# Splitting the last grouped FFN into three parts of token tiles and routing two of them inside the attention ahead of it

## The chip, the cores and the metric

The kernel runs on one core of one Trainium2 chip. The core has five engines that work from queues of their own, each in order: PE (matrix multiplication and transposes; its weight loads are listed apart as PEld), DVE (vector work), ACT (activation functions and copies), POOL (which also issues the indirect DMAs, those that scatter or gather rows by an index) and SP (which issues the plain DMAs). The metric is the time of one execution on the device, in microseconds (us). Three executions of the kernel before took 4240.65, 4247.43 and 4250.56 us, so the median is 4247.43 us.

## The reference, cut to what matters

The input is 8 sequences of 512 tokens of 256 numbers, 4096 tokens in all, in float32. Six blocks follow one another, each adding to the tokens: an expert FFN, a causal attention, the same expert FFN, a grouped FFN, a second attention without a mask, and the same grouped FFN again. The change concerns the last two:

```python
def _L1_attn_ref(x, w_q, w_k, w_v, w_o):            # 16 heads of 64
    q, k, v = (jnp.einsum('bsd,hdk->bhsk', x, w) for w in (w_q, w_k, w_v))
    weights = jax.nn.softmax(jnp.einsum('bhqk,bhmk->bhqm', q, k) * scale, axis=-1)
    z = jnp.einsum('bhqm,bhmk->bhqk', weights, v)
    ...
    return x + jnp.einsum('bse,ed->bsd', z, w_o)

def _L1_ffn_ref(x, gate_w, w1, w2, w3, ws1, ws2, ws3):
    weights, indices = _gate(xt, gate_w)             # 4 of 16 experts, from 2 of 4 groups
    ...
    a = jax.nn.silu(h1) * h3                         # each expert: 256 -> 128
    y = jnp.einsum('tei,eid,te->td', a, w2, c)       # only 4 of 16 in c are not zero
    z = jax.nn.silu(xt @ ws1) * (xt @ ws3) @ ws2     # a shared FFN for every token
    return (y + z).reshape(shape)

x = x + _L1_attn_ref(_layernorm(x, axis=-1), ...)
x = x + 0.5 * _L1_ffn_ref(_layernorm(x, axis=-1), ...)
```

## The kernel before

The tokens stay on chip in the tile `x`, as 32 token tiles of 128 tokens. Most of the text below is on two stages.

**The second attention** (`_attn1`) runs over 64 chunks n, 8 for each of the 8 sequences, each with two heads, and each in two halves g = 2n and 2n+1. A half computes scores, takes the maximum (DVE, L1110), the exponentials (ACT, L1117), divides (DVE, L1127), transposes (PE, L1139) and copies the transposes back (L202 on ACT, L204 on DVE). What doesn't belong to the chain of a chunk is cut into small pieces: the list `fill` holds projections, value products and the units of `Front`, and is emptied over the chunk; `own[n]` holds pieces that run at the end of chunk n (the statistics of layer normalisation, `moments`, and their end, `ln_finish`); `advance(steps, 1)` runs one more piece of a routing and is called six times a chunk. The order of the instructions of each engine is the order in which this code writes them, but for some statistics which the scheduler moves ahead.

**The grouped FFN** (class `Grouped`) sends each token's normalised row to four slots in DRAM, one for each expert chosen. Slots are collected into 144 slot tiles of 128 rows that have one expert each. The token tiles are dealt into parts, before 20 and 12 of them. For each part the routing (`routing`) finds experts, weights and slots: a long sequence of small DVE instructions with three PE matmuls in it (L1426, L1434, L1514), cut by `yield` into pieces. Then `send` (L1358, the DMA on L1364) issues four indirect DMAs a token tile. When all rows of a part have been sent, the slot tiles that these rows must fill can be computed, and `closed` says up to which tile that is. `ready` says how many tiles must be done and stored before the results of a part's tokens may be fetched. For parts of 20 and 12, `closed` is 0 and 65, and `ready` is 96 and 144.

**The steps.** `tile_steps` gives one step for each slot tile, 144, and four to empty the pipeline. A step transposes a tile (`turn`, L1768 `tpx`, copied by ACT to `xT`, L1770), multiplies the tile before it with its expert's weights (`hide`, L1786 `hs`, then ACT L1792 and DVE L1794), transposes that of three steps before (`back`, L1798 `tpa`, copied by ACT, L1800) and gives the result of four steps before (`give`, L1806 `yps`), which is copied out by ACT or DVE:

```python
            if j < self.closed[-1] and len(self.parts) > 2:

                nc.scalar.copy(ys["at"][:, i, :], yp)
            else:
                nc.vector.tensor_copy(ys["at"][:, i, :], yp)
```

Slot tiles come in by plain DMAs (`load`, L1752) in groups of up to four, and go out to DRAM by plain DMAs (L1818), all on SP's queue. A group of the next part is not loaded two groups ahead (L1780).

**The way back.** `collect` (L1571) makes a list of pieces. A piece issues one indirect DMA on POOL that gathers a tile of result rows (`gather`, L1546, tile `yg`, eight buffers, at most four transfers at a time), and adds the rows gathered two token tiles earlier to `x` (`add`, DVE, L1565). There are 128 gathers.

**The last stage** (`ffn1_after`) is what runs after the attention. It loads the weights, normalises and transposes the tiles of part 1 (`prepare`), and then runs the 148 steps. Beside each of the first ones two pieces of part 1's routing run, and at their end part 1's sends are written in one go, 48 of them. From step `f.ready[0] + 6` on, which is step 102, each step also takes one or two pieces of the way back. After the steps comes the tail: a `Pump` runs the shared FFN, 48 units (L1702 `hp`, L1724 `yp`), and takes pieces of the way back by the pattern on L2045, ten for six units, until none is left. Each token tile goes out when its shared part and its rows are in.

**Part 0** is prepared inside the attention by `Front`: `units` normalises a group of four tiles (POOL, L1354), transposes it and computes the gate's logits, and `send` normalises a tile again and sends it. The chunk after which this may begin is `begin = NC * groups + 2`, 42 for the 20 tiles: units in chunks 43 to 47, routing from chunk 48, one tile sent in each half of chunks 54 to 63.

Of the kernel before, what the change touches and what calls it, by code (L numbers as in the profile page):

```python
# [20 lines left out]
P = 128  # L21
# [40 lines left out]
class Kernel:  # L62
# [951 lines left out]
    def _attn1(self, ctx, weights, beside, after):  # L1014
# [169 lines left out]
            t = psum.tile([P, CH], F32, name="row", tag="m", bufs=3)  # L1184
            return t[:, :cols]

        known = []
        steps = after.routing(0, front.lg, front.pool, row_psum, lambda: known.append(True))
        groups = after.parts[0] // QT

        def moments(pool, stats, t):
            return lambda: self.ln_moments(pool, stats, t, 2)
# [2 lines left out]
        own = {}  # L1195
        for first, tiles, n in ((3 * QT, 2 * QT, 10), (5 * QT, 3 * QT, 25)):
            for t in range(0, tiles, 2):
                own[n] = moments(pool, stats, first + t)
                n += 1
            own[n] = lambda first=first, tiles=tiles: self.ln_finish(pool, stats, first, tiles)  # L1200

        begin = NC * groups + 2
        for t in range(0, after.parts[0], 2):
            own[33 + t // 2] = moments(front.pool, after.stats, t)
        assert len(own) == 4 + 6 + 2 + after.parts[0] // 2 and max(own) == begin
        last = own[begin]
        own[begin] = lambda: (last(), self.ln_finish(front.pool, after.stats, 0, after.parts[0]))

        E = mybir.EngineType
        with tc.manual_schedule(engines={E.PE, E.DVE, E.Activation, E.Pool}):  # L1210
            self.ln_range(pool, stats, 0, 3 * QT)
            for piece in sum(prepare(0), []) + heads(0) + heads(1):
                piece()
            exps, divide = scores(0)
            exps(1)
            divide(0)
            divide(1)
            fill, tail = [], []
            coming = prepare(1)
            for n in range(N):  # L1220
                b, c = divmod(n, NC)
                if c == 0:
                    coming = prepare(b + 1) if b + 1 < B else [[]] * NC
                if n + 2 < N:
                    fill += heads(n + 2)
                fill += coming[c]
                if 1 <= n - begin <= groups:
                    fill += front.units(n - begin - 1, row_psum)

                def rest():  # L1230

                    if beside:
                        beside.pop(0)()

                def ahead():

                    if n > begin + groups:
                        advance(steps, 1)

                for half in range(2):  # L1240
                    g = 2 * n + half
                    if g + 1 < 2 * N:
                        exps, divide = scores(g + 1)
                    if half == 0 and tail:
                        tail.pop(0)()
                    t = g - 2 * N + after.parts[0]
                    if t >= 0:
                        assert known
                        front.send(t)
                    turn(n, 2 * half)  # L1250
                    more = g + 1 < 2 * N
                    if more:
                        exps(1)
                    if half == 0 and tail:
                        tail.pop(0)()
# [12 lines left out]
                    rest()  # L1268
                    ahead()
                if n in own:  # L1270
                    own[n]()
# [659 lines left out]
class Front:  # L1931


    def __init__(self, k, f, ctx):
        self.k, self.f = k, f
        self.pool = ctx.enter_context(k.tc.tile_pool(name="front", bufs=1, reuse_waits="tile"))
        self.gw = self.pool.tile([P, DC, E1], F32, name="gw")
        k.nc.sync.dma_start(out=self.gw, in_=k.w["gate_wT"].rearrange("(c p) e -> p c e", p=P))
        self.lg = self.pool.tile([P, f.parts[0], E1], F32, name="chosen")
        self.xn = {}  # L1940

    def normal(self, t, n):
# [4 lines left out]
            self.f.rows(self.k.nc.gpsimd, self.xn[:, i, :], t - t % QT + i)  # L1947
        return self.xn

    def units(self, g, row_psum):  # L1950

        k, nc = self.k, self.k.nc
        xn = self.normal(g * QT, QT)
        xnT = self.pool.tile([P, DC, CH], F32, name="xnT")

        def column(c):
            def run():
                tp = row_psum(CH)
                for i in range(QT):
                    nc.tensor.transpose(tp[:, i * P : i * P + P], xn[:, i, c * P : c * P + P], k.ident)  # L1960
                k.evict(xnT[:, c, :], tp, c)
            return run

        def logits():
            lp = row_psum(CH)
            for c in range(DC):
                nc.tensor.matmul(
                    lp[0:E1, :], lhsT=self.gw[:, c, :], rhs=xnT[:, c, :], start=(c == 0), stop=(c == DC - 1)
                )
            lT = self.pool.tile([E1, CH], F32, name="lT")  # L1970
            nc.scalar.copy(lT, lp[0:E1, :])
            box.append(lT)

        def back():
            lg = row_psum(QT * E1).rearrange("p (t e) -> p t e", e=E1)
            for i in range(QT):
                nc.tensor.transpose(lg[:, i, :], box[0][:, i * P : i * P + P], k.ident[0:E1, 0:E1])
            nc.vector.tensor_copy(self.lg[:, g * QT : g * QT + QT, :], lg)

        box = []  # L1980
        return [column(c) for c in range(DC)] + [logits, back]

    def send(self, t):
        self.f.send(0, t, self.normal(t, 1)[:, t % QT, :])


def ffn1_after(k, f, out):
# [3 lines left out]
    rows_out = out.rearrange("(t p) d -> p t d", p=P)  # L1991
    with ExitStack() as ctx, k.tc.manual_schedule(engines={E.PE, E.DVE, E.Activation, E.Pool, E.SP}):
        f.enter(ctx)
        a = f.parts[0]
        load, step, total = f.tile_steps()
        f.expert_weights()
        load(0)
        f.shared_weights()
        part = f.prepare(1)
        while advance(part, 1):  # L2000
            pass
        part = f.route_and_send(1)
        left = {t: 2 for t in range(TT)}

        def done(t):
            left[t] -= 1
            if left[t] == 0:
                nc.sync.dma_start(out=rows_out[:, t, :], in_=k.x[:, t, :])

        coming = f.collect(done)  # L2010
        begin = f.ready[0] + 6
        rest, more = list(range(a // QT)), True
        for i in range(total):
            step(i)
# [36 lines left out]

def tile_kernel(tc, w, out):
    with ExitStack() as ctx:
# [89 lines left out]
```

## Time and profile before

| what | value |
|---|---|
| median of three runs | 4247.43 us |
| the profiled execution, its own time | 4227.88 us |
| its span, first to last instruction | 4226.2 us |
| busy: PE, DVE, ACT, POOL | 3723.0, 2115.9, 1484.4, 1203.4 us |
| mean granted clock of PE | 0.916 |
| score matmuls of the second attention | from 2528.9 us, the last chunk's at 3714.0 us |
| weights of the last stage are asked for | 3734.8 us |
| first slot tile of the last stage is transposed | 3764.3 us |
| first and last send of part 1 | 3802.0 and 3863.5 us |
| first and last gather of the last stage | 4006.9 and 4205.6 us |
| first shared matmul of the tail | 4108.0 us |

Times inside the execution are from its first instruction on. A busy time counts overlapping instructions once. "Idle before, releaser" in brackets is how long an engine had done nothing when an instruction began, and what seems to have ended that. "Issue" there means that the profile shows nothing waited for, "remote" that the event came from something it has no record of.

### The profile page before, as it was taken

Reading aid. Unit: us, or ns where it says so; the run is one execution under the profiler, and the core shown is the slowest. Engines: PE = TensorE matmul, PEld = TensorE weight load, DVE = VectorE, ACT = ScalarE, POOL = GpSimd, SP = SyncE. Lnnn points to the kernel's source line nnn. Section 1 sums busy time; section 2 is a strip of 40 time slices with the busy share of each in tenths; the row PEclk is TensorE's granted clock in tenths of the full one; section 3 lists DMA queues with packets and bytes.
Section 4 is the critical chain, followed back from the end, with each engine's and each line's share of the span. In section 5 each row is a group of like instructions: output and inputs, shape, how many; then the busy total and the mean of one; then the engine's idle time right before and its main releaser. Section 6 shows DMA issues by size and latency. Waiting matters only on the chain.

```text
span 4226.2 us, 51448 instructions
## 1 busy us (share of the span) xinstructions
PE 3723.0 (88%) x17088; PEld 2154.2 (51%) x17088; DVE 2115.9 (50%) x5708; ACT 1484.4 (35%) x3483; POOL 1203.4 (28%) x1098
## 2 busy tenths in 40 slices
PE   4999978999999499997567989999999999985987
PEld 2666643333334266664245764555554544554754
DVE  7122126554544622213442458786777678662354
ACT  3222223343343322222132435454454444442431
POOL 2433342232230143331533332210000113604065
PEclk7999988898896699999688999999999999997998
DMA  5333247200000323324222741000000000234453
GB/s 190 65 79 77 51 118 242 86 25 12 21 23 3 101 66 77 76 53 118 83 93 99 235 129 31 28 23 1 1 1 1 1 1 31 70 107 140 156 175 109
DMA packets 262995, 316.64 MB, mean 75 GB/s; under 512 B 31696, under 2 KB 232784, under 8 KB 262480
## 3 DMA queue, kind: packets, MB, share of 16 engines
q1 hardware_dynamic: 213584, 212.12, 15.7%
q0 software_dynamic: 49152, 101.24, 9.9%
q8 instruction: 142, 2.33, 0.2%
q14 instruction: 117, 0.96, 0.1%
HBM read 157.81 MB, written 147.06 MB: 72 GB/s over the span
## 4 chain that ended last, share of the span: by engine, by line
PE 64%; issue 13%; DVE 10%; ACT 5%; POOL 3%; another core or an unknown queue 3%; DMA 2%; SPq 0%; POOLq 0%; ACTq 0%; DVEq 0%
PE hs L1786 6%; PE hp L518 5%; PE op L531 5%; PE zp L1153 5%; PE sp L1105 5%; PE tp L1139 5%; PE pq L1080 4%; PE st L853 3%; PE yps L1806 3%; PE hp L1702 3%; PE yp L1172 3%; PE pv L1060 3%; POOL acc_d L538 2%; PE pp L721 2%
## 5 line engine op out<-in xcount | busy, mean ns | idle before, releaser
L1117 ACT ACTIVATE ex<-sp,nmax 128x512 f32<-128x512 f32 x512 | 344.8, 685 | 469.4 <-DVE nmax L1110 463.3
L531 PE MATMUL op<-w,hid 128*128 128x256 f32 x2048 | 456.2, 380 | 0.0
L518 PE MATMUL hp<-exT,w 128*128 128x512 f32 x1024 | 448.9, 597 | 0.0
L1546 POOL DMA_INDIRECT yg<-ys_d,slot x256 | 265.7, 1038 | 565.7 <-DMA ys_d<-ys 209.8
L531 PEld LDWEIGHTS op<-w,hid 128*128 128x128 f32 x2048 | 384.9, 190 | 57.0 <-issue 7.7
L1786 PE MATMUL hs<-w_sb,xT 128*128 (+1 forms) x1152 | 320.6, 403 | 61.3 <-ACT xT L1770 30.5
L538 POOL DMA_INDIRECT acc_d<-ob,idx x128 | 207.0, 1617 | 570.9 <-ACT ob L537 570.9
L536 DVE TENSOR_TENSOR ob<-op,b 128x256 f32<-128x256 f32 x128 | 54.4, 425 | 542.7 <-PE op L531 465.6
L1139 PEld LDWEIGHTS tp<-ident,ex 128*128 128x128 f32 x2048 | 228.7, 141 | 183.0 <-issue 107.5
L518 PEld LDWEIGHTS hp<-exT,w 128*128 128x128 f32 x1024 | 193.5, 191 | 232.3 <-issue 230.4
L824 DVE CUSTOM_DVE_ANT_0 junk<-sp,mask 128x128 f32<-128x128 f32 (+3 forms) x512 | 248.6, 485 | 124.9 <-PE sp L817 104.7
L1110 DVE TENSOR_REDUCE nmax<-sp 128x2 f32<-128x1024 f32 x256 | 300.3, 1215 | 17.8 <-PE sp L1105 16.5
L1139 PE MATMUL tp<-ident,ex 128*128 128x128 f32 x2048 | 279.4, 279 | 13.8 <-DVE eT L204 12.9
L522 ACT ACTIVATE hid<-hp,b 128x512 f32<-128x512 f32 x256 | 175.9, 687 | 323.0 <-PE hp L518 305.5
L1364 POOL DMA_INDIRECT slots_d<-wide,slot x176 | 173.4, 985 | 340.5 <-DVE lane L1501 232.3
L1105 PE MATMUL sp<-qk,qk 64*128 64x512 f32 x1024 | 257.4, 621 | 2.1 <-ACT ex L1117 2.1
L862 ACT ACTIVATE ex<-st 128x1024 f32<-128x1024 f32 (+3 forms) x256 | 174.2, 703 | 240.6 <-DVE st L860 240.4
L1786 PEld LDWEIGHTS hs<-w_sb,xT 128*128 128x128 f32 x1152 | 207.9, 201 | 93.0 <-ACT xT L1770 35.7
L1127 DVE TENSOR_SCALAR ex<-ex,rec 128x512 f32<-128x512 f32 x512 | 246.0, 523 | 8.8
L1080 PE MATMUL pq<-xnT,wide 128*128 128x512 f32 x512 | 241.7, 596 | 5.5 <-ACT qk L1086 5.5
L1794 DVE TENSOR_TENSOR as<-sgs,hs 128x128 f32<-128x128 f32 x288 | 82.5, 286 | 309.0 <-ACT sgs L1792 234.4
L1153 PE MATMUL zp<-eT,v 128*64 128x512 f32 x1024 | 234.9, 599 | 0.0
(346 smaller groups left out, 5866.7 us busy)
## 6 DMA issues: line engine op xcount, KB each, us to landing
xs<-slots_d SPq DMA_DIRECT2D x70, 512.0 KB
ys_d<-ys SPq DMA_DIRECT2D x70, 512.0 KB
w<-in_W SPq DMA_DIRECT2D x32, 1024.0 KB
slots_d<-mask SPq DMA_DIRECT2D x8, 2304.0 KB
ys_d<-mask SPq DMA_DIRECT2D x8, 2304.0 KB
w_sb<-in_w SPq DMA_DIRECT2D x24, 512.0 KB
xn_d<-xn SPq DMA_DIRECT2D x16, 512.0 KB
acc_d<-x SPq DMA_DIRECT2D x8, 1024.0 KB
```

What stands on the lines that cost most here:

```text
L518: nc.tensor.matmul(hp, lhsT=w1[:, c, f * P : f * P + P], rhs=exT[e][:, c, h * CH : h * CH + CH], start=(c == 0), stop=(c == DC - 1),)
L531: nc.tensor.matmul(op, lhsT=hid[h][:, f, i * P : i * P + P], rhs=w2[:, f, :], start=(f == 0), stop=(f == FC - 1),)
L538: inst = nc.gpsimd.indirect_dma_start(out=acc_d[:, :], out_offset=bass.IndirectOffsetOnAxis(ap=idx[:, e, st : st + 1], axis=0), in_=ob, in ...
L824: nc.vector.tensor_tensor_reduce(out=junk[:, :wd], in0=sps[h // 2][:, h % 2, :wd], in1=mask[:, S - wd :], scale=1.0, scalar=NEG, op0=ALU.a ...
L1080: nc.tensor.matmul(pp, lhsT=(wq, wk)[a][:, k, c * P : c * P + P], rhs=seq[b]["xnT"][:, k, :], start=(k == 0), stop=(k == DC - 1),)
L1105: nc.tensor.matmul(sp[:, j, :], lhsT=q[r, qt * P : qt * P + P], rhs=k[r, :], start=True, stop=True)
L1110: nc.vector.tensor_reduce(m, sp, AX.X, ALU.max, negate=True)
L1117: nc.scalar.activation(ch["ex", 2 * half + i][:, j, :], sps[i][:, j, :], AF.Exp, bias=nmax[i][:, j : j + 1], accum_out=sums[i][:, j : j + 1],)
L1139: nc.tensor.transpose(tp[:, k, :], ch["ex", qt][:, j, k * P : k * P + P], self.ident)
L1153: nc.tensor.matmul(zp[DK1 * j : DK1 * j + DK1, :], lhsT=seq[b]["v", h][:, k, at : at + DK1], rhs=ch["eT"][:, j, k, :], start=(k == 0), sto ...
L1546: inst = nc.gpsimd.indirect_dma_start(out=self.y[t, r], out_offset=None, in_=self.k.ys_d[:, :], in_offset=bass.IndirectOffsetOnAxis(ap=sel ...
L1786: nc.tensor.matmul(hp.rearrange("p a i -> p (a i)"), lhsT=st[j]["xT"][:, c, :], rhs=self.w13[:, st[j]["e"], c, :].rearrange("p e i -> p (e ...
```

## The change

The last grouped FFN gets three parts of 12, 8 and 12 token tiles. The first two are prepared inside the attention, each on its own schedule, and the third takes the place of the former part 1. `closed` becomes 0, 33 and 49, `ready` 65, 112 and 144. In the attention part 0 has its units in chunks 27 to 29, its routing from chunk 30 and its sends in halves 96 to 107; part 1 has its units in chunks 43 and 44, its routing from chunk 45 and its sends in halves 112 to 119. The statistics move to chunks 11 to 26 and 35 to 42. In the last stage the way back starts at the step that the next token tile's part allows: tiles 0 to 11 from step 71, tiles 12 to 19 from step 118, and tiles 20 to 31 after the steps. Because there are now more than two parts, the condition on L1812 quoted above holds for the first 49 slot tiles.

```diff
-        known = []
-        steps = after.routing(0, front.lg, front.pool, row_psum, lambda: known.append(True))
-        groups = after.parts[0] // QT
+        known, steps = {}, {}
+        ahead_of = [(h, NC * after.base[h + 1] // QT + 2) for h in range(len(after.parts) - 1)]
+        sends = {}
+        for h, begin in ahead_of:
+            steps[h] = after.routing(h, front.lg[h], front.pool, row_psum, lambda h=h: known.setdefault(h, True))
+        at = 2 * N - 4
+        for h, _ in reversed(ahead_of):
+            at -= after.parts[h] + 4
+            for t in range(after.parts[h]):
+                sends[at + t] = (h, t)
...
-        begin = NC * groups + 2
-        for t in range(0, after.parts[0], 2):
-            own[33 + t // 2] = moments(front.pool, after.stats, t)
+        for h, begin in ahead_of:
+            first, tiles = after.base[h], after.parts[h]
+            for t in range(first, first + tiles, 2):
+                n = NC * (t // QT + 1) + 2
+                own.setdefault(min(n + 1 + t % QT, begin), []).append(moments(front.pool, after.stats, t))
+            own[begin].append(
+                lambda first=first, tiles=tiles: self.ln_finish(front.pool, after.stats, first, tiles)
+            )
...
-                if 1 <= n - begin <= groups:
-                    fill += front.units(n - begin - 1, row_psum)
+                for h, begin in ahead_of:
+                    if 1 <= n - begin <= after.parts[h] // QT:
+                        fill += front.units(h, n - begin - 1, row_psum)
...
-                    if n > begin + groups:
-                        advance(steps, 1)
+                    for h, begin in ahead_of:
+                        if n > begin + after.parts[h] // QT:
+                            advance(steps[h], 1)
...
-                    t = g - 2 * N + after.parts[0]
-                    if t >= 0:
-                        assert known
-                        front.send(t)
+                    if g in sends:
+                        h, t = sends[g]
+                        assert h in known
+                        front.send(h, t)
...
-        part = f.prepare(1)
+        part = f.prepare(last)
...
-        begin = f.ready[0] + 6
         rest, more = list(range(a // QT)), True
+
+        def begin():
+
+            t = (TT + 2) - -(-len(coming) // TOPK)
+            return f.ready[sum(t >= b for b in f.base[1:-1])] + 6
+
         for i in range(total):
             step(i)
             more = more and advance(part, 2)
             if not more and rest and i % 4 == 0:
                 f.normal(rest.pop(0))
-            if i >= begin:
-                for _ in range(1 + i % 2):
+            for _ in range(1 + i % 2):
+                if i >= begin():
                     coming.pop(0)()
...
-        two = Grouped(k, 1, (20, 12))
+        two = Grouped(k, 1, (12, 8, 12))
```

More of the change, by code (lines that the diff above doesn't have):

```diff
@@ L1197, in _attn1 @@
             for t in range(0, tiles, 2):
-                own[n] = moments(pool, stats, first + t)
+                own.setdefault(n, []).append(moments(pool, stats, first + t))
                 n += 1
-            own[n] = lambda first=first, tiles=tiles: self.ln_finish(pool, stats, first, tiles)
-        begin = NC * groups + 2
-        for t in range(0, after.parts[0], 2):
-            own[33 + t // 2] = moments(front.pool, after.stats, t)
-        assert len(own) == 4 + 6 + 2 + after.parts[0] // 2 and max(own) == begin
-        last = own[begin]
-        own[begin] = lambda: (last(), self.ln_finish(front.pool, after.stats, 0, after.parts[0]))
+            own.setdefault(n, []).append(lambda first=first, tiles=tiles: self.ln_finish(pool, stats, first, tiles))
+        for h, begin in ahead_of:
[6 more added lines that the diff above has]
+            )
         E = mybir.EngineType
@@ L1269, in _attn1 @@
                     ahead()
-                if n in own:
-                    own[n]()
+                for piece in own.get(n, []):
+                    piece()
                 tail = products(n)
@@ L1938, in __init__ @@
         k.nc.sync.dma_start(out=self.gw, in_=k.w["gate_wT"].rearrange("(c p) e -> p c e", p=P))
-        self.lg = self.pool.tile([P, f.parts[0], E1], F32, name="chosen")
+        self.lg = [self.pool.tile([P, n, E1], F32, name=f"lg{h}") for h, n in enumerate(f.parts[:-1])]
         self.xn = {}
@@ L1948, in normal, with units @@
         return self.xn
-    def units(self, g, row_psum):
+    def units(self, h, g, row_psum):
         k, nc = self.k, self.k.nc
-        xn = self.normal(g * QT, QT)
+        xn = self.normal(self.f.base[h] + g * QT, QT)
         xnT = self.pool.tile([P, DC, CH], F32, name="xnT")
@@ L1977, in back, with send @@
                 nc.tensor.transpose(lg[:, i, :], box[0][:, i * P : i * P + P], k.ident[0:E1, 0:E1])
[L1978 removed]
+            nc.vector.tensor_copy(self.lg[h][:, g * QT : g * QT + QT, :], lg)
         box = []
         return [column(c) for c in range(DC)] + [logits, back]
[L1983 to L1984 removed]
+    def send(self, h, t):
+        self.f.send(h, t, self.normal(self.f.base[h] + t, 1)[:, t % QT, :])
 def ffn1_after(k, f, out):
@@ L1993, in ffn1_after @@
         f.enter(ctx)
-        a = f.parts[0]
+        last = len(f.parts) - 1
+        a = f.base[last]
         load, step, total = f.tile_steps()
@@ L1998, in ffn1_after @@
         f.shared_weights()
-        part = f.prepare(1)
+        part = f.prepare(last)
         while advance(part, 1):
             pass
-        part = f.route_and_send(1)
+        part = f.route_and_send(last)
         left = {t: 2 for t in range(TT)}
```

## The prediction

> **What bounds the kernel now.** I read the page first, then busy times by stretch of the span, then waits and timeline of the bad stretches. The page:
>
> ```profile
> span 4226.2 us, 51448 instructions
> ...
> PE 64%; issue 13%; DVE 10%; ACT 5%; POOL 3%; another core or an unknown queue 3%; DMA 2%; SPq 0%; POOLq 0%; ACTq 0%; DVEq 0%
> ```
>
> PE sets the end, but 16% of the chain is time that no instruction explains. Busy times by stretch show where (from:to, length, then busy us and instructions of PE, PEld, DVE, ACT, POOL; PE's clock, DMA share, GB/s):
>
> ```profile
> core 0: us, PE busy (x) PEld busy (x) DVE busy (x) ACT busy (x) POOL busy (x), PEclk, DMA share, GB/s
> 3103.40:3310.80 207.40, 206.44 (x970) 111.52 (x968) 154.00 (x298) 99.16 (x248) 4.71 (x2) 1.00 0.00 1
> 3440.00:3555.00 115.00, 105.70 (x465) 55.45 (x463) 95.80 (x198) 44.92 (x114) 10.74 (x9) 0.96 0.02 5
> 3764.30:3803.00 38.70, 31.37 (x148) 24.22 (x147) 31.23 (x115) 15.64 (x50) 0.98 (x1) 0.91 0.23 69
> 3812.00:3869.30 57.30, 15.14 (x37) 8.98 (x37) 4.48 (x13) 4.20 (x14) 39.61 (x41) 0.55 0.32 112
> 3869.30:4005.00 135.70, 130.87 (x696) 109.49 (x697) 56.16 (x171) 62.68 (x234) 0.00 (x0) 0.97 0.48 152
> 4005.00:4108.00 103.00, 85.89 (x403) 63.36 (x401) 55.86 (x154) 35.15 (x133) 67.62 (x65) 0.97 0.59 186
> 4108.00:4226.20 118.20, 94.90 (x290) 53.74 (x288) 50.41 (x113) 14.52 (x25) 65.72 (x64) 0.90 0.37 110
> ```
>
> Line by line: attention without extra work (PE full); attention with the routing of 20 tiles; first steps with part 1's routing; steps under its sends (PE 26% busy); undisturbed steps; steps with gathers; tail with gathers. PE is never the limit where POOL issues much in the last stage. There POOL is in the middle of two long waits:
>
> ```profile
> POOL yg L1546 <- DMA ys_d<-ys: 142.3, 1, 142.3
> POOL slots_d L1364 <- DVE lane L1501: 113.8, 1, 113.8
> ```
>
> POOL is idle for 113.8 us before the sends and 142.3 us before the gathers, then issues all it has. What that does to the others, from the timeline (start, length):
>
> ```profile
> 3849.40 0.63 PE L1768 MATMUL tpx<-ident,xs 128*128 128x128 f32 x2
> 3857.09 0.98 POOL L1364 DMA_INDIRECT slots_d<-wide,slot  x1 [0.30 <-issue]
> 3859.21 0.37 ACT L1770 COPY xT<-tpx 128x256 f32<-128x256 f32 x1 [10.99 <-remote]
> ...
> 4154.90 1.04 PE L1633 MATMUL tp<-ident,wide 128*128 128x128 f32 x8
> 4161.15 0.58 ACT L1636 COPY xnT<-tp 128x512 f32<-128x512 f32 x1 [10.75 <-remote]
> 4161.79 8.39 PE L1702 MATMUL hp<-xnT,ws_sb 128*128 128x512 f32 x14 [5.86 <-issue]
> ```
>
> PE ends a transpose at 3850.0 and ACT, which has nothing else to do, begins to copy it at 3859.2. In the tail the same takes 5.2 us. It happens while POOL issues one indirect DMA every 1.29 to 1.33 us without a pause, and not beside the 80 sends in the attention, where POOL rests after every four. I read it as: a wait that is not yet met is answered late while POOL streams.
>
> **What the Trainium skill says.** "TensorE: Matmul & The Clock Gate", section "What's actually happening": PE runs at half clock after an idle window of about 3.4 us and at full clock after a busy one. The clock records agree on two values, 0.50 and 1.00, but gaps of 2.0 and 2.7 us already brought half clock for 3 to 7 us here, so a gap costs up to 3.5 us more. "DMA: Bandwidth & Descriptors", section "SWDGE vs HWDGE vs iDMA": GpSimd writes the descriptors of its DMAs into rings in SBUF itself; it speaks of DVE hindering that, not of a stream hindering others, which the trace shows. "Perfetto Trace Analysis", section "Per-engine timelines": a semaphore's way to the other engines is outside the recorded instruction; the ACT line above fits, a wait with no recorded cause.
>
> **The change part by part**, against the profiled span of 4226.2 us.
>
> *Attention, routing.* Chunks 49 to 54 (3441.7 to 3574.0, by first score matmuls) took 132.3 us, the same places one batch earlier without routing (3120.0 to 3234.8) 114.8: the routing of 20 tiles costs 17.5 us. Of it 9.3 are PE gaps over 0.3 us, the worst 2.66 and 2.04, each with a clock dip (7 and 3 us at half speed, 5 us lost); its three PE matmuls are the rest. DVE's own time for it is 35.8 us in 85 instructions. For 12 tiles the last stage shows 28.2 us, for 8 the first grouped FFN 46.7 for two, so 23.4. DVE thus gets about 51 instead of 36 us, more in all, but in shorter pieces: the longest piece, L1486 and L1489 twice, falls from 2x(1.49+0.82) = 4.6 to 2x(0.83+0.55) = 2.8 us. If gaps follow piece length, 12 tiles leave about 5 and 8 tiles about 4 us of gaps, matmuls 3, dips 1.5 in place of 5: 13.5, that is -4. If they follow DVE's time, 17.5x51/35.8 = 25: +7.5. I take -4, since without routing DVE has 53 of 207 us free.
>
> *Attention, the rest.* Five units before and after, about 5 us each: 0. A second `ln_finish`, and six statistics before the one at chunk 26 (6x(0.41+0.18) = 3.5 us DVE): the first costs a 1.63 us gap at 3331, so +2. The 80 sends keep their four and a pause; before, chunks 54 to 56 with them were within 1 us of chunks without, and the one that lost more (3645 to 3672, a 2.60 us gap and a dip) waited for a late DVE copy. POOL's addition of chunk 48 now queues behind two sent tiles; only later projections read it: 0. Sum of the attention: -2.
>
> *First steps.* DVE is 31.2 of 38.7 us busy and late for PE three times (gaps of 2.03 before L1426, 1.32 before L1434, 2.28 before L1514, two of them with dips of 3 us at half speed, 1.5 lost each). Twelve result copies, 5.0 us of DVE, go to ACT, which is 15.6 us busy. Two gaps and their dips can go: 2.0+2.3+3.0 = 7.3 at most; I take -5. In exchange ACT has one more late wait a step under the sends. These 57.3 us saw only four steps; one fewer costs 1.63 us: +2. The 48 sends stay, and with them this stall. Sum: -3.
>
> *Undisturbed steps* stay at 1.63 us (tile 28 to tile 64 in 58.7 us). ACT then has 0.37+0.28+0.26+0.37 = 1.3 us a step: hidden. The new part's first load stalls tile 33 as it does tile 65 now (4.3 us gap), and the next change of part has its load four steps ahead, 6.5 us, against 4.7 from issue to use: 0.
>
> *Gathers beside steps.* 69 pieces are taken in 46 steps now, 80 in 54 then. The stretch of 103.0 us would take 41x1.63 for the full steps and about 5.5 for emptying, 72: 31 us lost for 65 gathers, 0.47 each, 6 of them at the end, where DVE works off its backlog before the tail. At 0.42 each 80 gathers cost 34; but POOL can catch up in the 15 steps between and the 8 after, and the backlog at the end is gone. If only POOL's pace counted (1.36x1.5 = 2.04 us a step), the loss would be 54x0.41 = 22. Ends -10 and +7; I take 0.
>
> *Tail.* PE's work at full clock is, with the lengths that the chain has for undisturbed groups, 8x7.13 (hp), 8x3.58 (yp), 5x1.04 transposes and 3.3 for the last output: 94.3 of 118.2, so 23.9 are lost beside 64 gathers. Afterwards 48 remain, since 80 are done. In proportion the loss is 17.9 (-6); by POOL's pace, 98 us for 64, 48 need 73.5 and PE's 94.3 becomes the limit (-24). I take -11.
>
> Sum: -2-3+0-11 = -16, so 4210 for the profiled span. Its own execution took 4227.9, 0.46% under the median of the runs shown, for which I have no reason; the median should move by the same: 4247.4-16 = **4231 us**.
>
> **The rivals.** *The tail stays as it is* (the stalls belong to the shared part's column transposes, which meet the same pattern of ten pieces in six units): its gain is 3, the sum -8, 4239. For it: up to the 32nd unit the pieces are the same as now; against it: POOL no longer starts ten gathers late. *POOL sets all three stretches*: loop -10, tail -20, first steps -5, attention -2: -37, 4210. For it: 1.33 us between gathers without any wait; against it: POOL waited 29.7 us for DVE's additions, so it isn't alone. *Slower: gathers between steps behave like the sends.* In the stall 41 sends cost 57.3-4x1.63 = 51 us, 1.24 each. The gathers of tiles 0 to 19 all lie beside steps now; at a price x they cost 80x in place of 31, and from x = 0.58 on this eats the 16 saved. At 0.75 it is 29 more: 4260. For it: it is the same instruction on POOL; against it: gathers, unlike sends, wait for DVE every few, and 0.47 was measured. *The change not doing what it says* would be tiles 12 to 19 fetched no earlier than the rest; the order written out excludes it, but 48 of 128 gathers do stay behind the steps.
>
> **How the numbers follow.** Forecast 0.50 (4220 to 4241), tail unchanged 0.18, POOL's pace 0.16, slower 0.16, into which falls the routing at +7.5. The range reaches over the third and half of the fourth: 4205 to 4256. 0.2%, 8.5 us, is about what can be told from no change. Faster: 0.48+0.06+0.16 = 0.70; within: 0.02+0.12+0.01 = 0.15; slower: 0.15.
>
> **What would show it.** Right: chunks 30 to 36 and 45 to 51 together lose under 17 us; DVE gaps before L1426 and L1514 in the last stage gone; the stall under the sends of 55 to 60 us still there; two groups of gathers with POOL idle between, steps at 2.0 to 2.2 us beside them; the tail near 107 us with 48 gathers. Wrong: steps of 2.5 us or more beside the first gathers, or a tail of over 115 us.

## The result, and the profile after

Five executions of the changed kernel took 4214.16 to 4225.13 us, median **4215.31**, against a median of 4250.56 for before, measured along with it: ratio 0.9926, interval 0.9908 to 0.9945. (Ratios here compare all executions of a set; they are not the quotient of the two medians.) Run again later beside many more executions of before, it came to 0.9998 (0.9978 to 1.0017, 22 executions against 45) and, on another chip, 0.9994 (0.9974 to 1.0014, 14 against 19). The executions of every kernel here, before and after alike, fall into two groups some 20 to 24 us apart, which part, in the traces of the three later chips, in a stretch of the first attention that the change doesn't touch; the first measurement set before's upper group against after's lower one. Like held against like, after is lower by 3 to 5 us in the first repetition (4213.9 for 4216.5 and 4235.7 for 4240.4, medians of the groups parted at 4228), and in the second 4 lower in one group and 2 higher in the other. So most of the first 35 us are not the change's. What is, is within 0.2%, and neither repetition tells it from nothing.

The span of after, and the chain's shares by engine. The chain of this execution could not be followed to its start (its shares add up to 84%), so the second line is that of the next trace of the same kernel, from the first set of the experiments:

```profile
span 4223.4 us, 51575 instructions
```

```profile
PE 62%; issue 13%; DVE 11%; ACT 5%; POOL 3%; another core or an unknown queue 3%; DMA 2%; SPq 0%; POOLq 0%; ACTq 0%; DVEq 0%
```

13% of "issue" and 3% of "unknown" are what before had: the change has not touched what no instruction explains. Busy times by stretch of after (columns as in the prediction: from:to, length, busy us and instructions of PE, PEld, DVE, ACT, POOL, then PE's clock, DMA share, GB/s):

```profile
3772.80:3801.80 29.00, 25.55 (x136) 20.37 (x136) 23.38 (x91) 17.75 (x58) 0.00 (x0) 1.00 0.29 92
3801.80:3879.50 77.70, 32.92 (x112) 22.54 (x111) 11.68 (x37) 14.05 (x49) 48.08 (x48) 0.60 0.34 117
3879.50:3955.90 76.40, 71.85 (x389) 60.01 (x388) 22.61 (x73) 41.74 (x156) 0.00 (x0) 0.98 0.48 154
3955.90:4112.50 156.60, 133.03 (x650) 103.99 (x649) 76.76 (x216) 57.06 (x216) 83.24 (x80) 0.95 0.59 183
4117.70:4223.40 105.70, 92.64 (x297) 53.34 (x295) 47.48 (x106) 15.02 (x26) 50.62 (x48) 0.95 0.35 105
```

In turn: steps 0 to 16; steps 16 to 28, under the last part's sends; steps 28 to 71, undisturbed; steps 71 to the last with the gathers; the tail. The first steps have lost their clock dips (1.00), the sends still hold PE to 33 of 77.7 us, and 80 of the 128 gathers now lie beside steps. POOL's long waits in the last stage (what for, us in total, times, longest):

```profile
POOL slots_d L1377 <- DVE lane L1514: 200.3, 1, 200.3
POOL yg L1559 <- DMA ys_d<-ys: 100.5, 2, 89.7
POOL yg L1559 <- DVE x L1578: 52.1, 31, 26.4
```

The wait for stored results, 142.3 us before, is now 89.7 us ahead of the first gather, and POOL pauses a second time, 26.4 us, after the 48th. POOL no longer does all its gathering late. The stall itself, from the timeline (start, length; in brackets idle time and its end):

```profile
3826.78 2.07 PE L1799 MATMUL hs<-w_sb,xT 128*128 x4 [1.83 <-issue]
...
3829.53 0.99 POOL L1377 DMA_INDIRECT slots_d<-wide,slot  x1 [0.30 <-issue]
3830.53 0.28 ACT L1805 ACTIVATE sgs<-hs 128x128 f32<-128x128 f32 x1 [3.81 <-remote]
```

PE was done at 3828.85, ACT had been idle since 3826.7 and begins at 3830.53: 1.7 us late, and the profile knows no reason but "remote". In steps 16 to 28 seven waits of ACT end in this way, 35 us in all, the most of them here (total, times, longest):

```profile
ACT sgs L1805 <- remote: 19.1, 3, 10.1
ACT xT L1783 <- remote: 10.6, 2, 5.3
```

The whole from the first score matmul of the second attention on, by starts of PE instructions. The two columns on the right are from the third and fourth set of the experiments, on two other chips, where the sends don't stall anything; the tail counts from its first shared matmul, which in before is at 4104.8 and not, as the text ahead of the result had it, at 4108.0.

| us | before | after | before, no stall | after, no stall |
|---|---|---|---|---|
| attention, first to last score matmul | 1192.0 | 1195.8 | 1191.9 | 1195.5 |
| from there to the first step | 43.5 | 44.1 | 43.5 | 44.2 |
| steps 0 to 16 | 33.6 | 28.9 | 33.5 | 28.9 |
| steps 16 to 28 | 79.7 | 77.7 | 24.9 | 24.1 |
| steps 28 to 71 | 77.0 | 76.4 | 77.2 | 89.1 |
| steps 71 to 143 | 144.4 | 156.6 | 128.3 | 130.1 |
| to the tail | 5.8 | 5.2 | 9.5 | 5.1 |
| tail | 121.3 | 105.7 | 107.8 | 96.9 |
| sum | 1697.3 | 1690.5 | 1616.6 | 1614.0 |

-6.8 us and -2.6 us: both lie inside the intervals of the repetitions.

One row depends on more than the change. In a third trace of before's attention (the first run of the second set, whose edit lies behind it) it took 1186.5 us, 5.4 less, with the instructions of PE, DVE and ACT in the same order: mainly chunk 49 with 1.5 us less, chunk 52 with 1.3 and chunk 59 with 2.9. There PE's clock fell for a shorter time or not at all. Chunk 52, in before and in that trace:

```profile
3519.45 1.59 PE L1139 MATMUL tp<-ident,ex 128*128 128x128 f32 x8 [2.04 <-DVE eT L204]
```

```profile
3405.08 1.25 PE L1139 MATMUL tp<-ident,ex 128*128 128x128 f32 x8 [2.04 <-DVE eT L204]
```

Behind the same gap of 2.04 us the clock records have 3.4 us at half speed in the first trace and none in the second. Against 1186.5 the change costs the attention 9 us instead of 4, and the sum of the two right columns would be +2.8 instead of -2.6.

### The profile page after: what moved, and what is told of

The parts are those of the page before. It is cut to its first block, busy times and chain, and to the rows that moved or that the text cites. A ratio compares the mean times of both kernels' runs of the same rounds, so it can differ in the third digit from the quotient of the medians.

```text
span 4223.4 us, 51575 instructions
## 1 busy us (share of the span) xinstructions
PE 3718.2 (88%) x17094; PEld 2151.2 (51%) x17094; DVE 2110.9 (50%) x5763; ACT 1500.4 (36%) x3536; POOL 1204.7 (29%) x1098
## 4 chain that ended last, share of the span: by engine, by line
PE 50%; issue 12%; DVE 10%; ACT 5%; POOL 3%; another core or an unknown queue 3%; DMA 1%; POOLq 0%; ACTq 0%; DVEq 0%
PE hs L1799 6%; PE zp L1153 5%; PE sp L1105 4%; PE pq L1080 4%; PE tp L1139 4%; PE st L853 3%; PE yps L1819 3%; PE pv L1060 3%; PE hp L1715 3%; PE yp L1172 2%; POOL acc_d L538 2%; PE pp L721 2%; PE tpx L1781 2%; ACT ex L862 1%
```

## The experiments

They came in four sets, each on another chip with its own executions of before. In the first set, whose chip stalls as that of the first measurement does, before took 4224.62 us (median of 45); in the others 4032.86 (67), 4029.45 (19) and 4035.49 (27).

### First set

*The changed kernel as it is.*

> The changed kernel once more, unchanged, as the measure for the runs beside it and for a second trace. The sum of steps that was predicted (-16 us) and the measured medians (-35 us) differ, while the two profiled spans differ by only 3 us. If the two first traces were unlike draws of the same spread, the ratio to the kernel before stays at 0.992 +- 0.002 and this trace shows which stretches vary from one execution to the next: I expect the stall under the 48 sends (steps 16 to 28, 77.7 us in the first trace) and the stretches with gathers to vary by several us, everything in the attention by under 1 us. If the size of the gain was a matter of the chip, the ratio moves to 0.996.

Measured 4218.58 us, ratio 0.9998 (0.9978 to 1.0017). Tail 109.0, steps 71 to 143 153.9 us. The first ratio is not repeated, the stretches are; the stall, expected to vary, took 77.5.

*VectorE copies the results of the first 49 slot tiles again, in the last stage only.*

```diff
-            if j < self.closed[-1] and len(self.parts) > 2:
+            if j < self.closed[-1] and len(self.parts) > 2 and self.n == 0:
```

> The changed kernel, but the results of the first 49 slot tiles of the last stage are copied out by DVE, as in the kernel before. Theory 1 (DVE was late for PE in the first steps): steps 0 to 16 take 33 to 34 us again in place of 29.0, the gap before the matmul L1439 comes back, the stall under the sends stays within 4 us of the changed kernel's, and the time is 3 to 6 us over it. Theory 2 (the copies don't matter, since the routing and the sends set this stretch): within 2 us of the changed kernel. Theory 3 (ACT's added late wait under the sends costs more than DVE's relief brings): 2 to 5 us faster than the changed kernel.

4225.47 us, 0.9999 (0.9976 to 1.0022). Steps 0 to 16 took 32.4 instead of 28.9 us, before 33.6: ACT's copies make 3.5 of the 4.7 us won there. Steps 16 to 28 took 79.2, so the stall doesn't ask who copies. In the total the difference is not to be seen.

*The first gathers not ahead of step 102.*

```diff
-            return f.ready[sum(t >= b for b in f.base[1:-1])] + 6
+            return max(102, f.ready[sum(t >= b for b in f.base[1:-1])] + 6)
```

> The changed kernel, but no rows are fetched before step 102, so that 69 pieces of the way back lie beside the steps and about 59 gathers are left for the tail, as in the kernel before. Theory 1 (the tail's loss is in proportion to the gathers that are left): tail of 116 to 120 us in place of 105.7, the stretch with gathers about 8 us shorter than the changed kernel's two, time +3 to +8 us over the changed kernel. Theory 2 (the stalls belong to the shared part's column transposes and to the ten-in-six pattern): tail within 4 us of 105.7 and the time not over that of the changed kernel. Theory 3 (fetching part by part is where the 35 us come from): +20 us or more.

4229.2 us, 0.9996 (0.9971 to 1.0021). Steps 71 to 143 fell from 153.9 (the changed kernel in this set) to 143.0 us, and the tail rose from 109.0 to 124.4 (the first theory had 116 to 120). So fetching early moves a loss more than it removes one: of the 15 us that it wins in the tail, where 48 instead of 65 gathers are left, 11 are lost beside the steps.

*A pause in the sends: GpSimd normalises one scratch row that nobody reads ahead of the four sends of each token tile, in the last stage only.*

```diff
             for t in range(self.parts[h]):
+                if self.n == 1:
+                    idle = self.route.tile([P, D], F32, name="idle")
+                    self.rows(self.k.nc.gpsimd, idle, self.base[h] + t)
                 self.send(h, t, self.xn[:, self.base[h] + t, :])
```

> The changed kernel, but POOL does one more vector instruction of about 1.2 us (normalising a row tile that nobody reads) ahead of each token tile's four sends in the last stage, so that its stream of indirect DMAs is broken after every four, as in the attention. Theory 1 (a wait that is not yet met is answered late while POOL streams without a pause): the 48 sends take 62 + 12 x 1.5 = 80 us, but the steps beside them run at 2 to 3 us, 16 to 28 in under 45 us, and the time falls by 30 to 45 us against the changed kernel. Theory 2 (each send costs the steps its 1.24 us, paused or not, for instance by its transfers): the stall stays at 75 us or more and the time is 0 to +18 us. Theory 3 (only a real wait of POOL, for a landing or for DVE, lets the others through): as theory 2.

4189.65 us (8 executions), ratio **0.9905** (0.9871 to 0.9939), though POOL has more to do: 29 us under the changed kernel of this set, where the first theory had 30 to 45. A scratch row in the timeline, then busy times of steps 16 to 28 and 28 to 71:

```profile
3793.13 1.22 POOL L1367 TENSOR_SCALAR idle<-x,mv,rstd 128x256 f32<-128x256 f32 x1
```

```profile
3784.20:3809.70 25.50, 22.84 (x112) 17.67 (x111) 11.90 (x37) 13.21 (x49) 18.56 (x17) 0.93 0.53 176
3809.70:3908.00 98.30, 75.71 (x389) 61.70 (x388) 23.80 (x73) 41.62 (x156) 43.98 (x43) 0.90 0.50 166
```

Steps 16 to 28 went from 77.7 to 25.5 us, with the same 112 matmuls on PE. No wait in them ends with "remote" any more, while the first grouped FFN of the same execution, whose sends got no pause, keeps its 19 (150 us). On this chip, then, the stall comes from sends without a pause, and neither from the traffic nor from POOL's time. 22 us come back in steps 28 to 71, where PE now waits for slot tiles (what for, total, times, longest):

```profile
PE tpx L1784 <- DMA xs<-slots_d: 21.0, 2, 16.8
```

The sends now run beside steps, the last at 3862.8, and the transpose of tile 49, the first that the last part's rows fill, can't begin before 3869.8. Whether it is POOL's own instruction or the 1.2 us that help was not tried.

### Second set, another chip

*The kernel before, with the same pause.*

> The kernel before with one thing added: in the last grouped FFN, GpSimd does one more LayerNorm row (about 1.2 us, into a scratch tile nobody reads) ahead of the four sends of each token tile. Theory 1, the stall under the last sends has nothing to do with the change but with sends that GpSimd issues without a pause: the stretch of steps 16 to 28 falls from 79.7 us to 25 to 35, the steps after it to 71 rise by about 20 since the sends run on beside them, and the last stage gets 25 to 35 us shorter (ratio about 0.993). Theory 2, the pause helped only because of where the changed kernel puts its twelve tiles: steps 16 to 28 stay above 60 us and the ratio stays above 0.997.

4030.11 us, ratio 1.0001 (0.9983 to 1.002). Steps 16 to 28 took 25.0 us, but this is not the pause's doing: here the same steps of kernels without it took 22.9 to 24.3, and 24.9 in before as it is (fourth set). Neither theory was tested. On this chip nothing stalls: no wait of its trace ends with "remote". The 190 us by which the whole is shorter lie in places of the same kind. In the first grouped FFN, which sends in the same way, the steps 0 to 36 took 122.6 us here and 178 to 183 in the first set, and from its first send to its first step 69 us for 112 to 115.

*One piece of the way back per step instead of one and a half.*

```diff
-            for _ in range(1 + i % 2):
+            for _ in range(1):
```

> The changed kernel, but the way back takes one piece per step instead of 1.5. Beside the gathers the steps 71 to 143 took 153.9 to 156.5 us against 129 for undisturbed steps (72 at 1.79 us), so 25 to 27 us for 80 gathers, 0.32 to 0.34 each. Theory 1, the cost comes from the pace of GpSimd's gathers: at one per step each costs about 0.18 us, and the stretch takes 143 to 148 us although it has about 90 gathers; the tail stays at 100 to 110 us; the end comes 5 to 12 us sooner. Theory 2, each gather costs the same whatever the pace: the stretch takes 155 to 161 us.

4020.49 us, ratio **0.9966** (0.9947 to 0.9985). Steps 71 to 143 took 118.4 us, 1.64 each, which is the length of an undisturbed step (1.63), so the 71 gathers beside them cost nothing; with 1.5 per step, and 76 gathers, they take 128.6 (the next run) to 130.1 (third set). Both theories were written for the chip that stalls and so were too high, but the first has the direction: here it is the pace. A gather occupies POOL for 1.04+0.30 us; 1.5 of them are 2.0 us a step, more than the step has; one fits. The tail stayed at 97.8 us.

*Units and routing of both parts one chunk later in the attention, statistics where they are.*

```diff
-                    if 1 <= n - begin <= after.parts[h] // QT:
-                        fill += front.units(h, n - begin - 1, row_psum)
+                    if 2 <= n - begin <= after.parts[h] // QT + 1:
+                        fill += front.units(h, n - begin - 2, row_psum)
...
-                        if n > begin + after.parts[h] // QT:
+                        if n > begin + 1 + after.parts[h] // QT:
```

> The changed kernel, but the units of both parts inside the attention (rows, transposes, logits) and the routing after them start one chunk later, the LayerNorm statistics staying where they are. In the changed kernel chunk 27, the first with units, took 27.9 us against 20.5 before. Theory 1, those 7 us are the wait for rows that GpSimd can only normalise after the statistics end one chunk earlier: chunk 27 falls back to 20 to 22 us, chunk 28 rises by what the units' own work costs (about 3 to 5), and the attention (1195.7 us) loses 3 to 7 us. Theory 2, the 7 us are the units' own work on TensorE and ScalarE: chunk 27 is short, chunk 28 takes 27 to 29 us, and the attention stays at 1194.5 to 1197 us.

4037.58 us, 1.0004 (0.9985 to 1.0023): not to be seen in the total. In the trace chunk 27 fell from 27.6 us (the run before this one) to 22.0, chunk 28 from 21.3 to 19.3, and the attention from 1196.3 to 1192.8, just inside what the first theory expected. In after the place looks like this:

```profile
3037.06 1.88 PE L1080 MATMUL pq<-xnT,wide 128*128 128x512 f32 x4
...
3037.35 4.85 POOL L1367 TENSOR_SCALAR xn<-x,mv,rstd 128x256 f32<-128x256 f32 x4 [50.86 <-PE tp L1139]
...
3043.47 3.78 PE L1080 MATMUL pq<-xnT,wide 128*128 128x512 f32 x4 [2.15 <-ACT qk L1086]
```

POOL can only normalise the four tiles once `ln_finish` is through, at 3037, and needs 4.85 us; the piece that transposes them stands in PE's and ACT's queues meanwhile. PE then runs at half speed: the same four matmuls take 3.78 us instead of 1.88.

*A pause ahead of the gathers of each of the first 20 token tiles, as with the sends.*

```diff
                 if t < TT:
+                    if then is not None and r == 0 and t < 20:
+                        idle = self.route.tile([P, D], F32, name="idle")
+                        self.rows(self.k.nc.gpsimd, idle, t)
                     self.gather(t, r)
```

> The changed kernel, but in the last stage GpSimd does one more LayerNorm row (about 1.2 us, into a scratch tile) ahead of the four gathers of each of the first 20 token tiles. Theory 1, gathers issued without a pause hold up the waits of other engines as the sends do: steps 71 to 143 fall from 153.9 to 156.5 us to 138 to 148, and the end comes 6 to 15 us sooner. Theory 2, the steps lose to something that a pause doesn't change (the adds on VectorE, the arrival of rows): steps 71 to 143 stay at 151 to 158 us and the end moves by less than 4 us.

4054.93 us, ratio 1.003 (1.0008 to 1.0051), slower, just clear of the interval. Steps 71 to 143 took 136.6 us: 6.5 more than the changed kernel in the third set. Where POOL's pace is the limit, a pause is more of the same: four gathers and a row are 4x1.34+1.2 = 6.6 us, 2.5 us a step, and the steps 96 to 104 took 2.6 on average. The first theory was not tested, since on this chip no wait is late; whether a pause helps the gathers on the first chip stays open.

### Third set, a third chip

*The changed kernel as it is.*

> The changed kernel as it is, once more. In one earlier set the kernel before took 4225 us and its steps 16 to 28 stalled 80 us under the sends; in the other it took 4033 us, and the steps 16 to 28 of changed kernels that had no pause took 23 to 24 us. Theory 1, the change gains about 11 us in the last stage (first steps and tail) and loses 4 to 10 in the attention (chunk 27 and the routing of the first part): within 0.2% of before in either set, ratio 0.998 to 1.001, and without the stall the steps 71 to 143 take 126 to 132 us. Theory 2, the first measurement (ratio 0.9926) holds: ratio below 0.995.

4025.77 us, 0.9994 (0.9974 to 1.0014). The first theory holds, with 130.1 us for steps 71 to 143.

*Three edits together: the one piece per step, the later units, the pause in both grouped FFNs (`if True:` in place of `if self.n == 1:`).*

> The changed kernel with three edits together: one piece of the way back per step instead of 1.5; the units and routing inside the attention one chunk later; a scratch row on GpSimd ahead of the four sends of every tile, in both grouped FFNs. Theory 1, each cures its own loss: where sends don't stall, the last stage's steps 71 to 143 take 117 to 121 us, the attention 1192 to 1194 us, and the ratio to before is 0.995 to 0.9975; where they stall, steps 16 to 28 of the last stage take 25 to 30 us, the first 36 steps of the first grouped FFN 120 to 150 us instead of 183, and the ratio is 0.965 to 0.985. Theory 2, the scratch rows cost what they save: no better than one piece per step alone (0.9966) where sends don't stall, no better than the pause in the last stage alone (0.9905) where they do.

4126.69 us, ratio 1.0246 (1.0221 to 1.0271). Neither theory had this. VectorE's waits in the first grouped FFN name it:

```profile
DVE x L1746 <- POOL idle L1367: 100.5, 14, 25.9
```

The scratch row reads `x`, and there VectorE already adds the shared FFN's outputs to the same tiles, so it must wait for POOL, which stands behind its sends. 100 us are the edit's own fault. In the last stage the pause cost 10.6 us (steps 28 to 71: 99.7 instead of 89.1) on a chip where it has nothing to cure.

### Fourth set, a fourth chip

*One piece per step and later units, no scratch rows.*

> The changed kernel with two of the three edits, one piece of the way back per step and the units one chunk later, and no scratch rows: in the run with all three, VectorE waited 100.5 us in the first grouped FFN until the scratch rows had read x, which is that run's own fault. Theory 1, both edits keep what they won alone: where sends don't stall, steps 71 to 143 take 117 to 121 us, the attention 1192 to 1194 us, and the ratio to before is 0.994 to 0.997. Where sends stall, steps 71 to 143 fall from 154 to 156 us to 120 to 140 and the ratio is 0.991 to 0.998. Theory 2, they stand in each other's way (later routing pushes the first gathers): the ratio is above 0.998.

4023.18 us, ratio **0.9971** (0.9954 to 0.9988), faster than before and, in its set, by more than the unedited change in any repetition, but not by more than the one piece per step alone (0.9966): the later units can't be seen in the total here either. Steps 71 to 143 (second line) take 117.9 us, in which PE is always busy; steps 28 to 71 stand ahead:

```profile
3702.50:3791.50 89.00, 74.68 (x388) 61.82 (x387) 22.61 (x73) 42.24 (x156) 33.29 (x34) 0.90 0.55 183
3791.50:3909.40 117.90, 117.90 (x649) 99.23 (x648) 72.13 (x208) 58.09 (x217) 71.97 (x71) 1.00 0.74 232
```

This pair was not run on a chip whose sends stall; there the pause in the last stage remains the best version measured.

*The kernel before as it is, for a second trace.*

> The kernel before as it is, for a second trace of it. Theory 1, what the change costs is seen wherever it runs: the attention takes 1186 to 1192 us against 1195.5 with the change, and where sends don't stall, the steps 28 to 71 take 77 to 80 us against 89.1 with the change, since before has 64 instead of 48 slot tiles to work on until the rows of the last part must have landed, and the first steps and the tail take about 13 us more than with the change. Theory 2, the wait at step 48 of the changed kernel has nothing to do with the number of parts: before shows a wait of 8 us or more at its own passage from one part to the next.

One execution. Its steps 16 to 28 and 28 to 71, and then the same of the changed kernel in the third set:

```profile
3701.60:3726.50 24.90, 22.28 (x111) 17.72 (x110) 16.84 (x52) 9.75 (x37) 14.79 (x16) 0.93 0.63 202
3726.50:3803.70 77.20, 72.41 (x388) 60.26 (x387) 32.13 (x99) 34.71 (x130) 32.53 (x33) 0.98 0.65 207
```

```profile
3702.00:3726.10 24.10, 22.02 (x111) 17.73 (x110) 11.79 (x36) 13.18 (x49) 15.60 (x15) 0.93 0.56 192
3726.10:3815.30 89.20, 75.73 (x389) 62.47 (x388) 22.78 (x73) 42.26 (x156) 32.50 (x33) 0.90 0.54 182
```

PE's work in the second lines differs by 3 us, the length by 12. PE's wait for slot tiles in it, in before and then in after:

```profile
PE tpx L1768 <- DMA xs<-slots_d: 4.3, 1, 4.3
```

```profile
PE tpx L1781 <- DMA xs<-slots_d: 13.1, 2, 8.2
```

4.3 us once (tile 65), against 4.9 (tile 33) and 8.2 (tile 49). Of these only the 8.2 us are a wait for rows: the last send began at 3769.3, the load of tile 49 at 3771.9, its transpose at 3776.8. In before the last send (3769.9) lies 17 us ahead of the load of tile 65 (3786.8). The first theory holds: where steps aren't held up by the sends, 49 slot tiles don't last until the rows of the last part are there, and 65 do.

## Why the prediction was right and wrong

It forecast 4231 us, from 4205 to 4256, and "faster", and the first measurement gave 4215. But its own sum was a difference, -16 us, and that turned out to be -7 in the traces of the first measurement and -3 to -5 in the like groups of the first repetition. So the range held, and the sum was two to five times too large. That the forecast came so near is in part luck: the attention and the gathers beside the steps were 6 and 12 us worse than forecast and the tail 5 better, and the measured 4215 owes most of its 35 us to unlike groups. Step by step:

- **Attention, routing, -4: wrong.** Both routings together cost what one did. Chunks 31 to 36 and 46 to 51 of after lost 17.3 us to the same places without routing; before's routing was put at 17.5 (14.7 in the trace with fewer half-clock stretches). Shorter pieces did not make smaller gaps in sum. With chunks 30 and 45, where the last unit ends, it is 21.7, over the bound of 17 that the prediction had named.
- **"Five units before and after: 0", and +2 for the second `ln_finish`: wrong by about 5.** Chunks 43 to 48 of before lost 25.9 us to their units; the three and two units of after, in chunks 27 to 30 and 43 to 45, lost 33. 7.4 of it is chunk 27, which begins right behind `ln_finish` and six statistics and then waits for POOL. Moving the units one chunk on takes about 3 us of the attention back. Chunk 59 gave 3 us, but not for its late copy: its gap is 2.23 us instead of 2.60, and what is gone is the 6.8 us at half clock behind it, which are missing in the third trace of before as well, behind a gap of 2.34. Sum +3.8 (+3.6 on the other chips) where -2 was forecast, and +9 against that third trace. Whether POOL's rows or ACT's queue set those 2 us gaps first was not separated.
- **First steps, -5: right.** 33.6 to 28.9, the gap before L1439 (formerly L1426) gone, the one before L1527 (formerly L1514) still 1.9 us but without a dip. The result copies are 3.5 of it.
- **The stall under the sends stays: right** on the chip of the first measurement, 77.7 us for 79.7. The reading of it, a wait answered late while POOL streams, has the run with the pause for it: 52 us and every "remote" gone from these steps. It is no property of the kernel alone, though; three chips don't show it.
- **Undisturbed steps, 0: right there, wrong elsewhere.** With the stall the steps under the sends last so long that all rows are sent by step 28, and 76.4 us match 77.0. Without it the same steps cost +11.9. What failed in the prediction is "the next change of part has its load four steps ahead, 6.5 us, against 4.7 from issue to use: 0": it asked how long a load takes, not when the rows that it loads are sent. Its other half, the 4 us at tile 33, was right. The cover was the stall; the pause, which takes the cover off, shows the same loss on the stalling chip.
- **Gathers beside steps, 0 between -10 and +7: wrong**, +12.2 and, repeated, +9.5. Fetching late again takes 10.9 back, so it is the 80 gathers' price. A sign of being wrong that the prediction had named was there: steps 80 to 88 took 2.66 us each (2.0 in the repetition). The catching up that was to pay for it didn't come: at 1.5 a step POOL needs 2.0 us, and it has its pause only after the first 48. On the chips without the stall it is +1.8, and there at one a step the whole loss of 12 us to undisturbed steps goes. On the first chip the steps lose 39 us; what the other 26 are was not found, since only 4.5 us of waits there end with "remote".
- **Tail, -11: right**, -15.6 and -12.3, and -10.9 elsewhere. With the gathers late again it returns to 124.4, so the 48 gathers instead of 65 make it.
- **The rivals.** "Slower: gathers between steps behave like the sends" has its mechanism in part (they cost more than was taken), at 39 us over 72 undisturbed steps for 80 gathers: 0.49 each, under the 0.58 that would have decided it. "POOL sets all three stretches" was right on POOL's pace beside the steps and wrong on the sign, since POOL had no time to give back there. "Tail unchanged" is out.

## What to carry to other kernels

When work is moved ahead, ask of each later load not how long it takes but what it must wait for, and what keeps that hidden now: here a stall hid that 16 fewer slot tiles were ready. Work beside a pipeline is free only while its engine's pace fits into a step; on the chips without the stall one gather of 1.34 us in a step of 1.63 cost nothing, 1.5 cost 12 us over 72 steps. And a gain of half a per cent from five executions a side is not yet a gain: repeat it on the same kernel and look whether the stretches of the trace add up to it.

## What the runs showed of the hardware that was not expected

- The same kernel took 4225 us on one chip and 4029 to 4035 on three others. POOL's records are the same on both kinds (a send of 0.98 to 0.99 us every 1.29), but only on the first does the rest of the core crawl beside them: 77.7 us for steps 16 to 28 against 24.1. Why is open. The profile's own sign is the releaser "remote": it ends 37 waits of ACT and DVE in before, 235 us in all, each of them beside or within 4 us of an indirect DMA of POOL, and not one in any trace of the other three chips. In the chain it is "another core or an unknown queue", 2 to 3% on the first chip and absent on the others.
- On that chip one POOL vector instruction of 1.2 us ahead of every four sends took 52 of the 78 us away.
- A gap of 2.15 us on PE was followed by half pace (3.78 us instead of 1.88), but its length doesn't decide: in chunk 52, with the same instructions in the same order, a gap of 2.04 us was followed by 3.4 us at half clock in two traces of before and by none in the third. With two places like it that makes 5.4 us in the attention without any change of the program there.
